# Heads of 8 in a gated four-layer block: weights times values on four column tiles, and a planner that knows VectorE's and POOL's shared port and the activation tables

## The chip, the cores and the metric

The kernel runs on one core of a Trainium2 chip. The metric is device time in microseconds (us) of that core; several runs are taken and their median is the kernel's time. Beside them one execution was recorded by the hardware profiler, and every duration of a single instruction comes from it.

## The reference

The input x is 16 batches of 128 tokens with 128 features; a context has 77 tokens with 96 features for each batch. Four layers follow one another, each a gated cross attention and a gated feed-forward part on the residual x:

- Layer 0: attention with 16 heads of 8 features, then a mixture of 8 experts of which each token takes 2 (gelu).
- Layer 1: attention with 16 heads of 64, then 8 linear experts weighted by a thresholded softmax.
- Layer 2: attention with one head of 128, then a mixture of 8 experts of which each token takes 1 (silu).
- Layer 3: attention with 16 heads of 8 again, then a feed-forward part with ternary weights, gelu and a layernorm.

The attention that the change touches (layers 0 and 3) is, for one batch:

```
q = (x @ wq + bq)  as 16 heads of 8        k, v = (y @ wk + bk), (y @ wv + bv)
attn = softmax(q k^T / sqrt(8), over the 77 context tokens)
out  = (attn v, heads side by side) @ wo + bo
```

The kernel works in float32 throughout.

## The kernel before, in words

**An order made by a planner.** The program is not emitted as it is written. Each call on an engine is recorded as an `Op` (`Program.record`, L200) with its inputs and outputs, an estimated duration (`_Engine.cost`, L457) and the engines that could run it; L441 is the one line through which nearly all of them are emitted, which is why the profile has nearly everything under L441 and why one goes by the names of tiles. `forward` (L251) then simulates the five engines: it repeatedly takes the ready operation with the smallest start time, plus a share of its duration for VectorE (`busy`), plus a small term for its place in the order (`bias`), if its tiles find free slots. `backward` (L351) turns the result round to get a new order, and `arrange` (L375) repeats both 8 times and keeps the shortest plan. The plan fixes engine, slot and order of every operation; the engines keep that order on the chip. Tiles of one tag share a fixed number of slots (L488), of which some are held back for older operations (`reserve`). The clock of TensorE is modelled (`_Clock`). The plan knows nothing of a port shared by VectorE and POOL, and nothing of ScalarE's loads of activation tables.

**Heads of 8** (`narrow_heads`, L741). Four groups of four batches. For a group: keys for all four batches in one product, spread by POOL into `kk`, in which each of the four heads of a 32-row band keeps its own 8 rows (a mask `hmask`); a layernorm of x (VectorE statistics, a power on POOL, `off_a` on VectorE, normalisation on VectorE or ScalarE), a transpose, the query product. For a batch, twice (halves `hf`, 8 heads each): two score products, one for each band of 32 rows (`sc`, 128 queries x 2 x 308 scores; 308 = 4 heads x 77); the maximum by head, the subtraction, and the exponential (`probabilities`, L668).

To multiply with the values, the weights have to be turned so that context tokens lie on partitions. 77 doesn't divide 128, so the subtraction writes its result split (`split`): first the tokens 0 to 63 of all 8 heads (512 columns), then the tokens 64 to 76 (104 columns), in two instructions. Four transposes of 128 columns give pairs of heads (`aT`), one of 104 the rest (`aTr`). The values lie in block matrices `vb` (`value_blocks`, L570, cleared once for each of the two layers by POOL; filled for each group by `narrow_values`, L714): a row for each token of a pair of heads, 9 columns for each head, the ninth being 1, so that the product gives the sum of the weights too. The product of weights and values (`av`, L795) has the turned weights as the stationary operand: 128 queries on partitions, five matmuls for each half, 10 for a batch. A reciprocal of 16 sums a row (`rs`) and one multiplication write `o`, four transposes a group turn it (`oT`), and the output product and a gated addition to x follow.

`narrow_values` loads the context in two arrangements (`ctxd`: tokens 0 to 63 twice; `ctxr`: tokens 64 to 76 eight times), one DMA of each for a group, in the queue of SyncE (SP), which also has the loads of the experts' columns and the stores of their results. For each batch two matmuls make the values, two copies put the first 64 tokens in place, one copy and a POOL multiplication with a mask (`rmask`) the rest.

Layer 0's groups are interleaved with its routing (L1503 to L1512); layer 3's with `ternary_ffn`, whose gelu needs another table than the exponential (L1539).

Of the kernel before, what the change touches and what calls it, by code (L numbers as in the profile page):

```python
# [11 lines left out]
F32 = mybir.dt.float32  # L12
# [15 lines left out]
KM = 64  # L28
KR = SK - KM
VW = 8 * 9  # L30
# [12 lines left out]
    ("cache", NE), ("hmask", 4), ("tri", NE * NE), ("rmask", 8),  # L43
# [102 lines left out]
class Op:  # L146
    def __init__(self, n, engines, us, after, order, size):
        self.n, self.engines, self.us, self.after, self.order = n, engines, us, after, order
        self.size, self.calls, self.deps, self.tiles = size, [], set(), []
        self.start = self.end = self.engine = None  # L150
        self.dense, self.streamed = 1.0, 0.0
# [26 lines left out]
class Program:  # L178
    LAG = {"tensor": 0.25, "vector": 0.08, "scalar": 0.08, "gpsimd": 0.1, "sync": 0.1}
    RATE = 290e3  # L180

# [18 lines left out]
    def record(self, engines, call, reads, writes, us, landing=0.0, group=None, size=0, streamed=0.0):  # L200
# [9 lines left out]
        op.streamed += streamed  # L210
        op.dense = min(1.0, op.streamed / max(op.us[0], 1e-3))
# [39 lines left out]
    def forward(self, order, ahead, bias, busy):  # L251
# [6 lines left out]
        holders = {tag: [None] * n for tag, n in self.slots.items()}  # L258
        held = {tag: [0.0] * n for tag, n in self.slots.items()}
        unplaced, out, wire, oldest = {}, [], 0.0, 0  # L260
        clock = _Clock()
# [28 lines left out]
        def place(op):  # L290

            at, got, taken = 0.0, [], {}
            for t in op.tiles:
                if t.slot >= 0:
                    continue
                frees = [
                    (held[t.tag][i], i) for i, h in enumerate(holders[t.tag])
                    if (h is None or h.left == 0) and i not in taken.get(t.tag, ())
                ]
                older = unplaced[t.tag][0] < t.nth  # L300
                if len(frees) <= (self.reserve.get(t.tag, 1) if older else 0):
                    return None
                when, i = min(frees)
                taken.setdefault(t.tag, set()).add(i)
# [4 lines left out]
        while len(out) < len(ops):  # L309
            best = None  # L310
            for n in ready:
                op = ops[n]
                got = place(op)
                if got is None:
                    continue
                if op.pos > oldest + ahead and got[1]:
                    if not any(t.left == 1 and t.slot >= 0 for t in op.tiles):
                        continue
                for e, when, us in zip(op.engines, op.when, op.us):
                    t = max(free[e], got[0], when)  # L320
                    key = (t + us * weigh[e] + bias * (op.pos - oldest), op.pos)
                    if best is None or key < best[0]:
                        best = (key, op, e, t, got[1], us)
# [5 lines left out]
            free[e] = op.end  # L329
            if op.after:  # L330
                wire = max(wire, op.end) + op.size / self.RATE
                op.end = wire + op.after
            for tl, i in got:
                tl.slot = i
                holders[tl.tag][i] = tl
# [7 lines left out]
            for tl in op.tiles:  # L343
                tl.left -= 1
                if not tl.left:
                    held[tl.tag][tl.slot] = max(u.end + self.LAG[u.engine] for u in tl.users)
# [28 lines left out]
    def arrange(self, rounds=8, ahead=300, bias=0.0008, busy=0.5):  # L375
# [23 lines left out]
    def emit(self, pools):  # L399
        order = self.arrange()  # L400
        with self.tc.manual_schedule():
            for op in order:
# [5 lines left out]
                for call in op.calls:  # L408
                    call(engine)

# [5 lines left out]
class _Engine:  # L416
# [5 lines left out]
    def __getattr__(self, what):  # L422
        def recorded(*args, group=None, covers=None, **kw):
# [24 lines left out]
            if self.names[0] == "tensor":  # L448
                moved, passes = (args[2], 1) if what == "transpose" else (kw["rhs"], 2)
                streamed = passes * n_of(moved) / 1200 * moved.shape[0] / 128  # L450
            return self.prog.record(
                self.names, call, reads, writes, us, costs[0][1], group, costs[0][2], streamed
# [4 lines left out]
    def cost(self, engine, what, args, kw, out):  # L457
        if "dma" in what:
            src = kw.get("in_", args[1] if len(args) > 1 else None)
            size = 4 * min(int(np.prod(v.shape)) for v in (out, src))  # L460
            if what == "indirect_dma_start":
                return 1.27, 2.2, 65536
# [6 lines left out]
        if engine == "gpsimd":  # L469
            if ALU.pow in args:  # L470
                return 0.8 + 0.06 * n, 0.0, 0
            return 0.12 + n / (1200 if what == "memset" else 440), 0.0, 0
# [4 lines left out]
        return 0.16 + n / 960 + (0.05 if what == "scalar_tensor_tensor" else 0.0), 0.0, 0  # L477
# [3 lines left out]
def tile_gated_blocks(  # L481
    ctx: ExitStack, tc: tile.TileContext, x, ctxa, ctxd, ctxr, cols, rows, b2s, emb, wqo0, wkv0, wx0,
# [6 lines left out]
        "sc": 2, "bank": 4, "large": 11, "middle": 18, "kk": 6, "at": 4, "aTr": 2, "other": 2, "mv": 3,  # L489
        "st": 4, "ve": 3, "rstd": 3, "mx": 4, "rs": 4, "rs1": 4, "rs2": 4, "junk": 2, "ys": 4,  # L490
        "back": 6, "wT": 1, "vr": 2, "off": 3,
    }
    reserve = {"sc": 1, "bank": 2, "large": 4, "middle": 6, "kk": 2, "at": 2}
# [62 lines left out]


    def pair_values(vb, par):

        flat = vb[KM * par : KM * (par + 1), 9 * par : 9 * par + 10 * VW]  # L560
        return flat.rearrange("p (c w) -> p c w", c=NH // 2)[:, :, :9]

    def rest_values(vb):

        flat = vb[: 8 * KR, : 10 * VW].rearrange("p (r w) -> p r w", r=2)[:, :, 4 * VW :]
        return flat.rearrange("p r (h d) -> p r h d", d=9)

    VB = 9 * VW + P

    def value_blocks(layer):  # L570
        whole = sb.tile([P, GB * VB], F32, tag="vb", name=f"vb_{layer}")
        nc.gpsimd.memset(whole, 0.0)
        got = []
        for i in range(GB):
            vb = whole[:, i * VB : (i + 1) * VB]
            for par in range(2):
                nc.gpsimd.memset(pair_values(vb, par)[:, :, 8:9], 1.0)
            nc.gpsimd.tensor_copy(
                rest_values(vb)[:, :, :, 8],
# [1068 lines left out]
```

## Time and profile before

| | us |
|---|---|
| three runs | 832.29, 835.16, 835.72; median 835.16 |
| profiled execution | 800.28 |
| its span, first to last instruction | 798.5 |
| granted TensorE clock | 0.944 of full speed |
| TensorE busy with matmuls | 701.5 |
| VectorE / ScalarE / POOL busy | 511.0 / 443.6 / 261.8 |
| ACT_TABLE_LOAD, 28 in all | 1.283 each |

The profiled execution took 34.9 us less than the median of the runs. A row of the profile's groups has the engine, the operation, the tile written and those read, the shape, the count, then the busy time in us and the mean of one in ns, then the idle time before it and what ended it. A matmul in float32 shows as two passes of TensorE (PE) with a weight load (PEld) each, a transpose as one. A row in order of time has the start, the duration and the number of instructions merged in it. By stages: layer 0's attention and routing lie at 0 to about 165 us, its experts to about 260, layers 1 and 2 to about 560, layer 2's experts to about 620, and layer 3 from there to the end.

### The profile page before, as it was taken

The page shows a single profiled execution, that of the slowest core. Times are in us where ns is not written, and L with a number is a line of the kernel's source. Part 1 is how long each engine was busy: PE and PEld are TensorE (multiplying, and loading weights), DVE is VectorE, ACT ScalarE, POOL GpSimd, SP SyncE. Part 2 cuts the span into 40 slices and gives each one's busy share as a digit, 9 for nine tenths or more (in the row PEclk, how much of TensorE's full clock was granted, in tenths as well). Part 3 has the DMA queues.
Part 4 walks back from the last instruction along what each step waited for, and adds up shares of the span by engine and source line. Part 5 has one row for each costly group of instructions (what it writes and reads, how often), then busy time and mean ns, then how long its engine had stood idle before and what let it go on. Part 6 is the DMA issues. An engine that isn't in the chain of part 4 may idle for free.

```text
span 798.5 us, 13848 instructions
## 1 busy us (share of the span) xinstructions
PE 701.5 (88%) x4848; PEld 555.7 (70%) x4848; DVE 511.0 (64%) x1462; ACT 443.6 (56%) x980; POOL 261.8 (33%) x327
## 2 busy tenths in 40 slices
PE   5699949999799998899899999878869977999886
PEld 3477837898687686568557767457859764867774
DVE  5868797482232664696769685675544796675864
ACT  3456525665456964565455555455636656556663
POOL 6511236107531222763322252461272260201010
PEclk9699969999999999999999999988989998979999
DMA  5005006387596100000000013500647100000000
GB/s 160 22 30 152 2 29 233 117 273 279 169 335 220 38 1 21 23 25 2 0 1 2 5 47 121 197 1 11 254 133 253 47 20 1 1 1 1 1 28 27
DMA packets 43541, 65.49 MB, mean 82 GB/s; under 512 B 4544, under 2 KB 32032, under 8 KB 43472
## 3 DMA queue, kind: packets, MB, share of 16 engines
q1 hardware_dynamic: 37520, 54.26, 20.6%
q0 software_dynamic: 3840, 9.31, 3.9%
q10 hardware_dynamic: 2112, 1.05, 0.5%
q8 instruction: 38, 0.62, 0.3%
q14 instruction: 31, 0.25, 0.1%
HBM read 52.41 MB, written 12.19 MB: 81 GB/s over the span
## 4 chain that ended last, share of the span: by engine, by line
PE 46%; DVE 10%; ACT 9%; issue 3%; POOL 2%; DMA 0%; POOLq 0%; ACTq 0%; DVEq 0%
PE sc_a L441 6%; PE aT_ps_a L441 6%; PE av_a L441 4%; PE oT_ps_a L441 4%; PE k_ps_a L441 4%; PE y_a L441 4%; PE y_ps L441 4%; PE y_f L441 3%; PE v_ps_a L441 3%; PE h_ps L441 3%; ACT L441 3%; DVE x L441 2%; POOL x L441 1%; ACT part_f L441 1%; PE h_ps_f L441 1%
## 5 line engine op out<-in xcount | busy, mean ns | idle before, releaser
L441 ACT ACTIVATE h<-h_ps,wx 128x128 f32<-128x128 f32 x304 | 86.4, 374 | 62.6 <-PE h_ps L441 52.6
L441 DVE TENSOR_REDUCE mx_a<-sc_a 128x8 f32<-128x616 f32 (+1 forms) x100 | 77.6, 776 | 28.6 <-PE sc_a L441 27.3
L441 ACT ACTIVATE at_a<-at_a 128x616 f32<-128x616 f32 (+1 forms) x100 | 70.4, 707 | 45.3 <-DVE at_a L441 42.9
L441 ACT COPY aT_a<-aT_ps_a 128x512 f32<-128x512 f32 (+1 forms) x124 | 70.1, 583 | 43.9 <-PE aT_ps_a L441 42.8
L441 DVE TENSOR_TENSOR at_a<-sc_a,mx_a 128x104 f32<-128x104 f32 (+3 forms) x164 | 83.9, 534 | 9.4 <-issue 4.0
L441 PE MATMUL h_ps<-rowsT,wx 128*128 128x128 f32 x608 | 83.9, 286 | 5.5 <-ACT h L441 3.4
L441 PE MATMUL aT_ps_a<-ident,at_a 128*77 128x128 f32 (+1 forms) x528 | 81.3, 288 | 6.3 <-ACT at_a L441 4.6
L441 PEld LDWEIGHTS h_ps<-rowsT,wx 128*128 128x128 f32 x608 | 77.0, 200 | 10.5 <-ACT h L441 4.8
L441 PE MATMUL y_ps<-wx,h 128*128 128x128 f32 x608 | 79.3, 278 | 3.7 <-DVE y L441 1.4
L441 PEld LDWEIGHTS aT_ps_a<-ident,at_a 128*77 128x77 f32 (+1 forms) x528 | 63.8, 150 | 24.6 <-ACT at_a L441 8.0
L441 PEld LDWEIGHTS y_ps<-wx,h 128*128 128x128 f32 x608 | 73.7, 194 | 7.0 <-DVE rowsT L441 1.6
L441 PE MATMUL av_a<-vb,aT_a 128*128 128x128 f32 x512 | 74.9, 293 | 2.3 <-ACT aTr_a L441 2.3
L441 PEld LDWEIGHTS av_a<-vb,aT_a 128*128 128x128 f32 x512 | 68.4, 207 | 8.3 <-ACT aTr_a L441 3.4
L441 PE MATMUL sc_a<-kk_a,q_a 32*128 32x308 f32 (+1 forms) x288 | 55.6, 492 | 16.8 <-DVE at_a L441 13.5
L441 POOL DMA_INDIRECT sorted_x<-xn_f,idx_f x48 | 46.7, 972 | 63.3 <-DVE r_both_f L441 29.8
L441 POOL TENSOR_TENSOR at_a<-at_a,rs_a 128x616 f32<-128x616 f32 x32 | 39.0, 1224 | 80.7 <-DVE rs_a L441 42.5
L441 POOL DMA_INDIRECT back_f<-sorted_y,idx_f x48 | 46.3, 965 | 57.3 <-DMA cf_a<-in_ctxd 26.1
L441 DVE TENSOR_TENSOR y<-y_ps,wx 128x128 f32<-128x128 f32 x76 | 21.5, 288 | 58.4 <-PE y_ps L441 27.9
L441 POOL TENSOR_TENSOR rstd_f<-ve_f,nhalf 128x4 f32<-128x4 f32 x16 | 16.3, 1019 | 112.2 <-DVE ve_f L441 104.1
L441 POOL TENSOR_TENSOR vb<-vr_a,cols_sb 104x128 f32<-104x128 f32 x32 | 14.0, 440 | 101.8 <-ACT vb L441 43.0
L441 PE MATMUL k_ps_a<-ctx_sb,wide_w 96*128 96x308 f32 x128 | 39.7, 446 | 5.8 <-ACT part_f L441 4.1
L441 PEld LDWEIGHTS sc_a<-kk_a,q_a 32*128 32x128 f32 (+1 forms) x288 | 23.6, 201 | 29.9 <-issue 10.4
(283 smaller groups left out, 1370.9 us busy)
## 6 DMA issues: line engine op xcount, KB each, us to landing
wx<-in_wx SPq DMA_DIRECT2D x60, 578.0 KB, 6.8
sorted_y<-y SPq DMA_DIRECT2D x76, 64.0 KB, 1.6
rows<-sorted_x SPq DMA_DIRECT2D x6, 512.0 KB, 3.9
sorted_x<-zero POOLq DMA_DIRECT2D x2, 1472.0 KB
cf_a<-in_ctxd SPq DMA_DIRECT2D x8, 224.0 KB
rows<-sorted_x SPq DMA_DIRECT2D x4, 448.0 KB
co_a<-in_ctxr SPq DMA_DIRECT2D x8, 182.0 KB, 3.6
x<-in_x ACTq DMA_DIRECT2D x4, 256.0 KB
```

What stands on the lines that cost most here:

```text
L441: getattr(engine, f)(*(_real(a) for a in args), **done)
```

## The change

In the attention with heads of 8:

- The 4 x 77 = 308 pairs of head and token of one 32-row band (four heads) stay in natural order: `probabilities` subtracts in one instruction again, and the 308 columns are turned in chunks of 128, 128 and 52 (`CHUNKS`). For a batch that makes 8 transposes of 128 columns as before and four of 52 instead of two of 104; the last four are evicted as one 52 x 512 copy.
- The values become the stationary operand, 32 columns wide (4 heads x 8 features), masked so that each row counts for its own head only; each band has one of four column tiles of TensorE, that is 32 partitions of the output. The sums of the weights come from a second product with the mask itself (`own`). For a batch: 2 x 3 chunks x 4 tiles = 24 matmuls. The output has features on partitions already, so `o` and its transposes are gone. The reciprocal now covers 128 elements a row, and the multiplication writes `oT`.
- `narrow_values` loads, for each batch, the context repeated over the 308 rows (`ctx4`, 112 x 384, one DMA a batch), makes the values with three matmuls, evicts them in one copy of 384 elements and masks them on POOL (384 elements). `value_blocks` is gone. Tag "v3" (9 slots) holds context, values and masked values.

In the planner: operations on POOL (other than DMA), and those of VectorE that read or write no PSUM and whose name begins with tensor or scalar (not tensor_reduce), can't overlap in the plan; an activation of another table than the last starts 1.28 us later; when nothing fits the reserves, the oldest operation may go without them. `rounds` 8 to 16, `bias` 0.0008 to 0.002, `busy` 0.5 to 0.3; some estimated durations; "middle" has 15 slots in place of 18.

```diff
-    def probabilities(scores, n, scale, name, split=None):
+    def probabilities(scores, n, scale, name):
...
+        nc.vector.tensor_tensor(at_v, scores, wide, ALU.subtract)
         nc.scalar.activation(at, at, AF.Exp, scale=scale)
...
+    def narrow_values(g, wv, n):
+        got = []
         for b in range(GB):
+            at = (g * GB + b) * PK
+            cx = sb.tile([KP, 3 * P], F32, tag="v3", name=f"cx_{n}_{b}")
+            nc.sync.dma_start(cx, ctx4[:, at : at + 3 * P])
+            vp = mm_tile(f"v_ps_{n}_{b}")[:, : 3 * D]
...
+            vr = sb.tile([P, 3, 4, 32], F32, tag="v3", name=f"vr_{n}_{b}")
+            evac(vr, vp.rearrange("p (c k d) -> p c k d", c=3, k=4))
+            vb = sb.tile([P, 3, 4, 32], F32, tag="v3", name=f"vb_{n}_{b}")
...
+            nc.gpsimd.tensor_tensor(vb, vr, mask, ALU.mult)
...
+                with nc.together(1.4):
+                    for sums in range(2):
+                        for c in range(3):
+                            for k in range(4):
+                                a = (chunks[k] + [aT[:, k, :]])[c]
+                                w = ones_of[:, c, :] if sums else vbs[b][:, c, k, :]
+                                nc.tensor.matmul(
+                                    av[32 * k : 32 * k + 32, sums * P : (sums + 1) * P],
+                                    lhsT=w[: a.shape[0]], rhs=a, start=(c == 0), stop=(c == 2),
+                                )
+                rs = sb.tile([P, S], F32, tag="rs", name=f"rs_{n}_{b}")
+                nc.vector.reciprocal(rs, av[:, P : 2 * P])
+                nc.vector.tensor_tensor(oT[:, b, :], av[:, :P], rs, ALU.mult)
...
+                        if e in op.port:
+                            t = max(t, port)
+                        if op.table not in (None, table):
+                            t += self.LOAD
...
-    def arrange(self, rounds=8, ahead=300, bias=0.0008, busy=0.5):
+    def arrange(self, rounds=16, ahead=300, bias=0.002, busy=0.3):
...
-        "sc": 2, "bank": 4, "large": 11, "middle": 18, "kk": 6, "at": 4, "aTr": 2, "other": 2, "mv": 3,
+        "sc": 2, "bank": 4, "large": 11, "middle": 15, "kk": 6, "at": 4, "v3": 9, "mv": 3,
```

## The prediction

> **What bounds the kernel now.** I read the engine shares first, then the chain of work that ended last, then the groups by shape, and last the order of time in two short stretches.
>
> ```profile
> PE 701.5 (88%) x4848; PEld 555.7 (70%) x4848; DVE 511.0 (64%) x1462; ACT 443.6 (56%) x980; POOL 261.8 (33%) x327
> ...
> PE 46%; DVE 10%; ACT 9%; issue 3%; POOL 2%; DMA 0%; POOLq 0%; ACTq 0%; DVEq 0%
> PE sc_a L441 6%; PE aT_ps_a L441 6%; PE av_a L441 4%; PE oT_ps_a L441 4%; PE k_ps_a L441 4%; PE y_a L441 4%; PE y_ps L441 4%; PE y_f L441 3%; PE v_ps_a L441 3%; PE h_ps L441 3%; ACT L441 3%; DVE x L441 2%; POOL x L441 1%; ACT part_f L441 1%; PE h_ps_f L441 1%
> ```
>
> TensorE is the bound, but not wall to wall: 88% counts overlapping passes. Summing, from the starts in the trace, what lies between one pass's streaming (0.85 ns a column) and the next start gives about 169 us in which no matmul streams; 19 of them lie before 40 us, 14 in the routing at 100 to 120, 15 at 640 to 680. So there are two kinds of time to win: TensorE's streaming in the attention with heads of 8, and gaps that the order leaves. The nameless ACT entry (3%; 2.7% in the chain's own answer, so 21.6 us) is table loads.
>
> An fp32 matmul shows as two passes. This is the product of values and weights of the kernel before, in order of time:
>
> ```profile
> 44.38 1.06 PE L441 MATMUL av_a<-vb,aT_a 128*128 128x128 f32 x8
> 45.27 0.39 PE L441 MATMUL av_a<-vb,aTr_a 104*128 104x128 f32 x2
> ```
>
> Eight passes start in 45.27-44.38 = 0.89 us, 0.111 each. A batch has 10 matmuls, 20 passes: 2.22 us, 71 us in 32 batches. The chain holds av_a for 4.4%, 35 us: half of it is on the path. The wide heads already put a product on two column tiles:
>
> ```profile
> 276.85 1.09 PE L441 MATMUL oT_ps_a<-aT_a,v_a 77*64 77x128 f32 x16
> 277.87 0.66 PE L441 MATMUL aT_ps_a<-ident,at_a 128*77 128x128 f32 x4
> ```
>
> Sixteen passes of the same 128 columns in 1.02 us: 0.064 each with entry and exit, so two tiles do run side by side. Inside the group the starts come in pairs, every 0.109 us.
>
> **VectorE's rows.**
>
> ```profile
> L441 DVE TENSOR_TENSOR at_a<-sc_a,mx_a 128x512 f32<-128x512 f32 x64 | 43.5, 680 | 0.1
> ...
> L441 DVE TENSOR_TENSOR at_a<-sc_a,mx_a 128x616 f32<-128x616 f32 x32 | 25.2, 788 | 1.2
> ...
> L441 DVE TENSOR_TENSOR at_a<-sc_a,mx_a 128x104 f32<-128x104 f32 x64 | 16.9, 265 | 8.0 <-issue 4.0
> ...
> L441 DVE RECIPROCAL rs_a<-av_a 128x16 f32<-128x16 f32 x32 | 8.1, 254 | 31.6 <-PE av_a L441 31.4
> ...
> L441 DVE RECIPROCAL rs_a<-rs_a 128x8 f32<-128x8 f32 x32 | 6.5, 203 | 1.1
> ```
>
> The reciprocal is the row to stare at: 203 ns for 8 elements a row, 254 for 16, 164 for 2: 6.4 ns for each further element, where the subtraction pays about 1.
>
> **VectorE against POOL, and table loads.**
>
> ```profile
> 25.04 5.21 DVE L441 SCALAR_TENSOR_TENSOR off_a<-mv_a,rstd_a 128x4 f32<-128x4 f32 x1
> 30.18 0.68 DVE L441 TENSOR_TENSOR at_a<-sc_a,mx_a 128x512 f32<-128x512 f32 x1
> ```
>
> ```profile
> 24.33 1.26 POOL L441 TENSOR_TENSOR x<-x,bos 128x512 f32<-128x512 f32 x1
> 25.55 2.24 POOL L441 TENSOR_TENSOR kk_a<-kr_a,cols_sb 128x1232 f32<-128x1232 f32 x1
> 27.76 2.47 POOL L441 TENSOR_TENSOR x<-x,bos 128x512 f32<-128x512 f32 x2
> ```
>
> ```profile
> L441 ACT ACT_TABLE_LOAD x27 | 34.6, 1283 | 1.3 <-PE h_ps L441 0.9
> ```
>
> A four-element operation (163 ns as a rule) lasts 5.21 us and ends when POOL's run ends at 30.23; behind it the next subtraction, and TensorE, stand (PE waits 5.8 us for at_a there). Over the run, VectorE's operations are 25 us longer than the usual time of their own shape in off_a (12.8), xn_a (5.6), x<-back (5.1) and ve_a (2.1).
>
> **What the skill says.** The Trainium skill, SBUF — State Buffer, "Who interferes with whom": a VectorE instruction with two SBUF inputs contends with a GpSimd one that reads SBUF, and the loser blocks fully; the 5.21 us agree. VectorE: DVE Perf Modes, "First, the fixed hardware budget": reciprocal is an iterative divide with a repeat count of 8; 6.4 ns an element agrees in kind. TensorE: Matmul & The Clock Gate, Part 3, "Measured speedup vs the span model": three column tiles of 32 gave 2.38 times; the trace shows two tiles only. ScalarE: Activation LUTs, "What ACT_TABLE_LOAD costs": 1283 ns and a drain of about as much; the row has the 1283, the drain no row shows.
>
> **The change part by part** (per batch, 32 batches; the sum is against the profiled 800.28 us, span 798.5).
>
> 1. *Product on four tiles.* 24 matmuls, 48 passes. If four run at once: 12 x 0.109 = 1.31 instead of 2.22: -0.91. Bounds: two at once 2.62, none 5.2. I take four: the two-tile group overlaps fully from its first pair. Transposes of the rest go from 2 to 4: +0.22; value projection from 4 passes to 6: +0.22; the transpose of o (4 a group) goes: -0.11; entering and leaving tile mode: after the tiled score group at 41.43 us the next weight load starts 0.09 us late and its pass takes 0.05 longer, and the load at entry has nothing to hide under: +0.2. Sum -0.38, 12 us in all; half on the path, like av_a now: **-6** (bounds +24 with pairs, worked out below, and -12).
> 2. *VectorE.* Two subtractions become one: 680+265-788 = 157 ns, twice: -0.31. The reciprocal goes from 16 to 128 elements: 254 + 112 x 6.4 = 0.97 us, +0.72. The product with it stays 290 ns. Net +0.40, 12.8 us. The planner prices the long reciprocal at 0.17+128/960 = 0.30, so each comes 0.67 late in a strict queue; behind it stand the next maxima and subtractions, and for those ScalarE's exponentials. VectorE has a third of slack in these stages (131 of 198 us busy after 600), so I put 0.4 on the path: **+5** (0 to +19).
> 3. *Evictions.* Values: 218+213+265 ns become one of 384 elements, about 480 between the 265 (128) and 583 (512) of ScalarE's rows: -0.22. The rest of the weights: 371 to 583: +0.21. oT: 583 a group: -0.15. **-1**; ScalarE and VectorE share it.
> 4. *POOL.* The masking goes from 128 elements (440 ns) to 384; 1232 take 2259, so 1.65 ns an element: 860 ns, +13.5 us. Gone are the clears of the value blocks (5.4+1.7+1.5 us), which ended at 5.6 us, before x arrives at 6.7: no gain there. POOL is 33% busy: **0**; uncovered, the first group pays 4 x 0.42.
> 5. *DMA.* 8 loads of 224 KB and 8 of 182 become 32 of 168: 2.1 MB more, 8 us of wire at the 279 GB/s of a full slice, and 16 more issues in SP's queue, each waiting for one of 9 slots; behind a waiting one stand expert columns and stores of y. Covered by loading ahead: **+1** (0 to +6).
> 6. *Planner, VectorE and POOL apart:* of the 25 us, 40% on the path (5.8 at 25 us and 3.6 at 650 are seen there): **-10** (0 to -25; it may also hold back work that never collided).
> 7. *Planner, table loads:* 28 now. One to start, gelu, exp, silu, exp, and two for each of four groups at the end make 13. I let 10 go, 12.8 us, 60% on the path (21.6 of 35.9): **-8** (0 to -15).
> 8. *Fewer buffers* ("middle" 18 to 15), other weights, more rounds: unknown, -10 to +10, taken as 0.
>
> Sum -6+5-1+0+1-10-8 = -19: 781 us profiled. The runs' median of 835.16 lies 34.9 above the profiled execution; I carry that over: **816 us**.
>
> **The rivals.**
> - *The tiles run only in pairs.* A matmul's two passes share a tile, so a queue that looks one instruction ahead finds only one neighbour. For: the trace shows no more than pairs. Against: with two tiles it couldn't show more. Then av costs 24 x 0.109 = 2.62, TensorE +0.93 a batch, 30 us, now as the bound 0.8 on the path: +24. With the other terms (-13): +11, **846**, slower. It decides from av = 2.22+0.67-0.53 = 2.36 us a batch (0.67 x 32 x 0.8 = 17 eats the 13 and the 0.5%).
> - *The reciprocal is on the path* whole: 23-4 = +19 instead of +5: **830**. For: each batch's tail runs through it, and the queue is strict. Against: VectorE's third of slack.
> - *The planner wins nothing*, its new estimates don't come true, and the smaller pools cost 10: -1+10: **844**.
> - *The planner wins all:* -25 and -15 instead of -10 and -8: **794**. For: 169 us of gaps.
>
> **The numbers.** Forecast 0.46 (own range 802 to 830), all won 0.19, reciprocal 0.15, pairs 0.11, planner nothing 0.09. A measurement here can tell about 0.5%, 4.2 us. Faster: 0.455+0.19+0.10 = 0.745, say 0.75. Same: 0.005+0.05+0.03 = 0.08. Slower: 0.10+0.07 = 0.17. The range 788 to 842 leaves out 0.07 below and 0.12 above.
>
> **What would show it.** av in order of time: 48 passes in about 1.5 us confirm step 1, 2.6 the pairs. RECIPROCAL rs_a 128x128 near 970 ns, and waits of mx_a or at_a behind it, step 2. off_a near 163 ns and no 5 us wait of PE, step 6. The count of table loads near 18, step 7. Gaps of TensorE before 40 us and at 640 to 680 still there would refute 6 and 7; SP waiting on v3 slots, step 5. The prediction is wrong if av is over 2.36 us, or if the new order opens gaps elsewhere.

## The result, and the profile after

The kernel after takes 831.04 us (median of 20 runs, 824.6 to 841.7), the kernel before 835.64 beside it (20 runs, 830.65 to 843.05): a ratio of 0.9938, 95% interval 0.9908 to 0.9967. The forecast was 816. The direction held; the size did not: a gain of 5 us where 19 were summed.

One thing has to be known of the numbers below. Chips differ: the kernel before takes 801 to 803 us on two of those used here and 835 on a third and in the runs shown. Its profiled execution (800.28) fits the faster kind alone, since none of its 20 executions beside the kernel after is under 830; the profile of after (826.01) is of the slower kind. The two pages can therefore not be subtracted from one another; ratios and profile pairs are taken within one kind of chip.

The page of after, its engine shares and its chain of what ended last:

```profile
PE 710.9 (86%) x5840; PEld 534.8 (65%) x5840; DVE 513.9 (62%) x1364; ACT 429.4 (52%) x932; POOL 272.3 (33%) x302
...
PE 68%; DVE 14%; DMA 5%; issue 4%; ACT 3%; another core or an unknown queue 3%; POOL 2%; DVEq 0%; POOLq 0%; SPq 0%; ACTq 0%
```

TensorE is still the longest, the nameless ACT entry (table loads) has left the chain, and 5% of DMA is new in it. The product of values and weights of one batch, in order of time (start, duration, matmul passes merged):

```profile
60.54 0.65 PE L462 MATMUL av_a<-aT_a,vb_a 128*32 128x128 f32 x16
61.12 0.42 PE L462 MATMUL av_a<-aTr_a,vb_a 52*32 52x128 f32 x8
61.47 0.64 PE L462 MATMUL av_a<-aT_a,own 128*32 128x128 f32 x16
62.04 0.42 PE L462 MATMUL av_a<-aTr_a,own 52*32 52x128 f32 x8
62.40 0.66 PE L462 MATMUL aT_ps_a<-ident,at_a 128*128 128x128 f32 x4
62.53 0.96 DVE L462 RECIPROCAL rs_a<-av_a 128x128 f32<-128x128 f32 x1 [0.66 <-PE av_a L462]
```

From the first of the 48 passes to the next other work are 1.86 us (60.54 to 62.40), where 20 passes took 2.22 and step 1 had 1.31 with 0.2 for entering and leaving. The groups that the prediction named (count, busy us, mean ns, idle before):

```profile
L462 DVE TENSOR_TENSOR at_a<-sc_a,mx_a 128x616 f32<-128x616 f32 x96 | 76.1, 794 | 5.8 <-PE aT_ps_a L462 1.1
...
L462 POOL TENSOR_TENSOR vb_a<-vr_a,own 128x384 f32<-128x384 f32 x32 | 32.8, 1033 | 51.9 <-ACT vr_a L462 33.9 <-DVE vr_a L462 15.4 <-PE v_ps_a L462 2.2
L462 DVE RECIPROCAL rs_a<-av_a 128x128 f32<-128x128 f32 x32 | 30.6, 956 | 26.7 <-PE av_a L462 26.6
...
L462 ACT ACT_TABLE_LOAD x17 | 21.8, 1283 | 4.4 <-PE h_ps L462 4.1
...
L462 DVE SCALAR_TENSOR_TENSOR off_a<-mv_a,rstd_a 128x4 f32<-128x4 f32 x16 | 2.6, 160 | 6.6 <-POOL rstd_a L462 6.6
```

Read one by one they say that the change does what it was said to do: one subtraction of 794 ns, a reciprocal of 956 (970 were estimated), 18 table loads (17 and one on another line) where there were 28, and off_a back at 160 ns with no 5 us stall in it. The prices on VectorE were about right; the product (1.86 us) and POOL's masking (1033 ns instead of 860) were priced too low. The larger question is what the operations are worth where they stand.

### The profile page after: what moved, and what is told of

It is laid out like the page before. It is cut to its first block, busy times and chain, and to the rows that moved or that the text cites. A ratio compares the mean times of both kernels' runs of the same rounds, so it can differ in the third digit from the quotient of the medians.

```text
span 824.0 us, 15717 instructions
## 1 busy us (share of the span) xinstructions
PE 710.9 (86%) x5840; PEld 534.8 (65%) x5840; DVE 513.9 (62%) x1364; ACT 429.4 (52%) x932; POOL 272.3 (33%) x302
## 4 chain that ended last, share of the span: by engine, by line
PE 68%; DVE 14%; DMA 5%; issue 4%; ACT 3%; another core or an unknown queue 3%; POOL 2%; DVEq 0%; POOLq 0%; SPq 0%; ACTq 0%
PE sc_a L462 8%; PE aT_ps_a L462 8%; PE av_a L462 8%; PE h_ps L462 7%; PE y_ps L462 6%; PE v_ps_a L462 6%; PE k_ps_a L462 5%; PE y_a L462 4%; PE oT_ps_a L462 4%; DMA wx<-in_wx 4%; PE y_f L462 3%; DVE x L462 2%; PE aTr_ps_a L462 2%; PE h_ps_f L462 2%
## 5 line engine op out<-in xcount | busy, mean ns | idle before, releaser
L462 PE MATMUL h_ps<-rowsT,wx 128*128 128x128 f32 x608 | 90.4, 302 | 29.6 <-DVE y L462 10.4
L462 PEld LDWEIGHTS h_ps<-rowsT,wx 128*128 128x128 f32 x608 | 83.1, 214 | 34.7 <-DVE y L462 11.9
L462 ACT COPY aT_a<-aT_ps_a 77x512 f32<-77x512 f32 (+1 forms) x118 | 66.7, 583 | 63.8 <-PE aT_ps_a L462 61.1
L462 DVE TENSOR_REDUCE mx_a<-sc_a 128x8 f32<-128x616 f32 (+1 forms) x100 | 77.6, 777 | 21.8 <-PE sc_a L462 21.4
L462 PE MATMUL y_ps<-wx,h 128*128 128x128 f32 x608 | 84.2, 291 | 5.8 <-DVE y L462 4.6
L462 PEld LDWEIGHTS y_ps<-wx,h 128*128 128x128 f32 x608 | 78.8, 205 | 8.8 <-issue 6.1
L462 DVE TENSOR_TENSOR at_a<-sc_a,mx_a 128x616 f32<-128x616 f32 (+1 forms) x100 | 78.0, 782 | 6.0 <-PE aT_ps_a L462 1.1
L462 PE MATMUL sc_a<-kk_a,q_a 32*128 32x308 f32 (+1 forms) x288 | 51.8, 468 | 16.3 <-DVE at_a L462 12.6
L462 POOL TENSOR_TENSOR vb_a<-vr_a,own 128x384 f32<-128x384 f32 x32 | 32.8, 1033 | 51.9 <-ACT vr_a L462 33.9
L462 DVE RECIPROCAL rs_a<-av_a 128x128 f32<-128x128 f32 (+1 forms) x40 | 31.8, 795 | 28.9 <-PE av_a L462 28.7
L462 PE MATMUL sc_a<-kk_a,xnT_a 128*128 128x308 f32 x128 | 38.5, 430 | 0.3 <-issue 0.2
```

The costliest lines, as they stand in the source:

```text
L462: getattr(engine, f)(*(_real(a) for a in args), **done)
```

## The experiments

The order on every engine is the planner's, and any edit that it can see (an operation, a price, a rule) makes it draw up a new one. All times are medians in us; the kernel before ran beside each.

| chip | before | kernel | us | ratio (95%) |
|---|---|---|---|---|
| one | 803.23 | b_again (before unchanged) | 802.09 | 0.9999 (0.9971 to 1.0027) |
| one | | planner_only | 763.77 | 0.9520 (0.9473 to 0.9566) |
| one | | heads_only | 812.62 | 1.0151 (1.0091 to 1.0212) |
| one | | recip_priced | 782.05 | 0.9763 (0.9710 to 0.9815) |
| two | 801.15 | planner_only_2 | 764.48 | 0.9548 (0.9511 to 0.9586) |
| two | | heads_only_2 | 811.76 | 1.0117 (1.0059 to 1.0174) |
| two | | after_3 (whole change) | 789.06 | 0.9874 (0.9833 to 0.9915) |
| two | | recip_priced_2 | 783.15 | 0.9790 (0.9747 to 0.9833) |
| two | 803.21 | planner_only_3 | 764.16 | 0.9508 (0.9459 to 0.9557) |
| two | | planner_long | 783.66 | 0.9761 (0.9714 to 0.9807) |
| two | | plan_no_port_2 | 795.67 | 0.9896 (0.9842 to 0.9949) |
| two | | plan_no_table_2 | 783.65 | 0.9740 (0.9701 to 0.9779) |
| one | 802.76 | planner_nudged | 780.29 | 0.9725 (0.9668 to 0.9782) |
| one | | after_nudged | 803.39 | 1.0029 (0.9999 to 1.0059) |
| three | 834.94 | after_again (whole change) | 828.52 | 0.9916 (0.9888 to 0.9944) |
| three | | recip_copy | 824.04 | 0.9880 (0.9827 to 0.9933) |
| three | | plan_no_port | 833.73 | 0.9985 (0.9958 to 1.0011) |
| three | | plan_no_table | 829.54 | 0.9933 (0.9914 to 0.9953) |

### The two parts apart

*b_again* is the kernel before, *planner_only* has the change's planner, estimates and weights with the attention and the buffers of before, *heads_only* the reverse:

```diff
 # planner_only                        # heads_only
-    def forward(...)   # of before    -    narrow_heads, narrow_values, probabilities   # of before
+    def forward(...)   # of after     +    narrow_heads, narrow_values, probabilities   # of after
```

> The kernel before, unchanged, for a second profile of it. Theory 1 (the profiled 800 us was a rare, lucky execution, in which the experts' columns came in time): its usual profile spans about 833 us, and the 33 us stand in the two expert stages as waits of TensorE for loads, so that the stage from the first gelu to the wide heads lasts some 125 to 140 us instead of 113. Theory 2 (the gap is the clock or something outside the program): the span is about 833 us with every stage longer by the same 4%.

> Only the planner's part of the change (shared port, tables, new weights, rounds and estimates), with the attention of before. Theory A (my sum: planner -18 us, attention -1): 0.975 to 0.985 of before. Theory B (the new orders give back in the expert stages what the attention wins): 1.00 to 1.02, with the table loads down to about 18 and the long off_a gone all the same.

> Only the attention's part (four column tiles, one subtraction, long reciprocal, 32 loads of context), planned by the planner of before. Theory A: 0.995 to 1.005, TensorE's gain and the reciprocal cancelling. Theory B: 0.97 to 0.985, the attention being the gain and the new planner the loss. Theory C (the reciprocal, priced by the planner at a third of its time, is the loss): 1.00 to 1.02.

The first says what one profile of the kernel before is worth: 802.09 us beside 803.23, with a profiled span of 806.3, so neither of its theories held, and the 34.9 us between profile and runs that I carried over were a difference between chips. The other two split the result: the planner alone wins 39.5 us (0.952, outside both of its theories), over twice the 18 that steps 6 to 8 gave it, and the attention part costs 9.4 (in Theory C's range) where steps 1 to 5 gave it a gain of 1.

That had to be repeated with the whole change on the same chip: *after_again*, meant for chip one, fell on chip three, and so the whole change had run only where the kernel before takes 835 us:

> The planner's part of the change with the attention of the kernel before, once more, on the same chip as the whole change and the attention part alone. On a chip where the kernel before took 803 us it stood at a ratio of 0.952. Theory A (the two parts get in each other's way: the attention part costs about 1.5%, and it spoils the plan as well): the ratio is 0.95 to 0.96 on this chip too, and the whole change stands 3% or more above it. Theory B (the gain of the planner's part depends on the chip, because the chips differ in what the stages of the experts take): on a chip where the kernel before takes about 835 us the ratio is 0.97 to 0.99, and the whole change stands at most 1.5% above it. Rival: the plan of this kernel is lucky on that one chip, and the ratio is here within 0.5% of 1.

> The attention part of the change with the planner of the kernel before, on the same chip as the whole change. It stood at a ratio of 1.015 where the kernel before took 803 us. Theory A (its cost comes from the order that it brings, not from the chip): 1.01 to 1.02 here too. Theory B (chip decides): within 0.5% of 1, or under it. If the parts add, the whole change is the product of this ratio and that of the planner's part alone; if they spoil one another the whole change is over 1% above that product.

> The whole change, unchanged, on the same chip as its two parts. If the parts add, its ratio is the product of theirs: with those of the earlier chip 0.952 x 1.015 = 0.966. It stood at 0.994 and at 0.992 where the kernel before took 835 us. Theory A (the parts spoil one another): 0.985 or more, and over 1% above the product of the two parts measured here. Theory B (chip decides): within 1% of the product of the two parts measured here, whatever that is.

> The changed kernel, unchanged, on the chip of these experiments, where the kernel before takes 803 us instead of 836. If the planner's part and the attention's part only added up (0.952 and 1.015), it is at 0.967. If the attention's long reciprocal upsets the new plan in particular, it stays near the 0.994 of the result. If the result's chip is what held it back (slower loads of expert columns), it falls between 0.965 and 0.98 and TensorE's gaps at 140 to 200 us shrink from 45 us in four slices of 20 to some 15.

The planner's part: 36.7 us won; the attention part alone: 10.6 lost; both: 12.1 won. The ratios of the parts multiply to 0.966, the whole stands at 0.987. So on top of the new planner the attention part costs 24.6 us (3.2%), not 10.6: in these orders the parts do not add. The chip is not the explanation, as all three were measured on chip two. Whether the parts get in each other's way, or three orders merely fell differently, this comparison can't tell; the section on the draw comes back to it.

Where the time is lost shows in the trace when the span is cut in three: to the first expert product of layer 0 (attention with heads of 8, and routing), from there to the last expert product of layer 2, and the rest (layer 3, heads of 8 again). Busy time of each engine by stretch (start and end, length, then busy us and instructions of TensorE, its weight loads, VectorE, ScalarE and POOL, then the granted clock of TensorE, the DMAs' share and GB/s), first planner_only_2:

```profile
0.00:131.20 131.20, 117.76 (x804) 92.26 (x805) 99.67 (x298) 70.39 (x154) 53.99 (x76) 0.95 0.33 108
131.20:616.20 485.00, 438.93 (x3091) 351.53 (x3089) 286.73 (x860) 260.33 (x634) 174.04 (x216) 0.95 0.31 101
616.20:766.90 150.70, 138.96 (x957) 107.90 (x956) 110.91 (x304) 94.57 (x181) 31.99 (x35) 0.94 0.05 15
```

and after_3, the whole change on the same chip:

```profile
0.00:137.60 137.60, 117.23 (x1307) 76.61 (x1307) 109.59 (x260) 69.62 (x132) 61.74 (x66) 0.94 0.36 111
137.60:623.10 485.50, 435.67 (x3054) 348.73 (x3055) 281.00 (x840) 257.15 (x625) 167.51 (x198) 0.94 0.31 101
623.10:786.40 163.30, 145.22 (x1482) 98.51 (x1480) 124.46 (x267) 102.31 (x176) 43.03 (x39) 0.93 0.08 22
```

The profiled spans differ by 19.5 us: 6.4 in the first stretch, 12.6 in the last, 0.5 between. Two profiles of one kernel scatter too: planner_only_3, the same kernel on the same chip as planner_only_2, has 134.5, 481.2 and 150.0, so only the last stretch stands clear. VectorE has 9.9 and 13.6 us more to do at the two ends and 5.7 less in the middle.

TensorE's side has to be counted from the starts. At 0.85 ns a column, as in the prediction, its passes stream 588.8 us in planner_only_2 and 576.5 in after_3, 12.3 less. But the time between the first pass and the last in which none streams grows from 163.3 us to 195.5, and it has two parts. Gaps under 150 ns, mostly the passes' own, grow from 71.5 to 84.2, by 12.7; the longer ones from 91.7 to 111.3, by 19.6. So the streaming that the four tiles saved was taken back by short gaps, and TensorE needs as much as before (660.3 and 660.7 us; 659.9 and 660.1 in the two kernels of the section on the draw). Where these gaps lie shows in one batch: the tiled product's first pass starts 0.20 us after the pass before it instead of 0.11 (medians), and it then takes 1.85 us against 2.23, which leaves 0.28 of the 0.71 us that were forecast. The attention's other passes (two transposes and two value passes more, one transpose less) take about as much, 0.33 us by the prediction's own prices.

The long gaps are as large as the loss in time, and some of them are slow passes: the granted clock is recorded at full speed or at half, and at half passes of 128 columns start 213 ns apart instead of 112 (medians of passes in a row in after_3). planner_only_2 spends 76.7 us at half, after_3 96.7; what they stream there would take 32.2 and 40.5 us at full, so some 8 us more are lost that way (an estimate from these figures; 6 against planner_only_3). Whether the clock falls because TensorE waits, or for another reason, no run separates. One place of the waits is visible in the score products, which wait for VectorE to give their PSUM buffer back. In planner_only_3:

```profile
L463 PE MATMUL sc_a<-kk_a,q_a 32*128 32x308 f32 (+1 forms) x288 | 55.6, 485 | 7.5 <-DVE at_a L463 7.5
```

and in after_3:

```profile
L462 PE MATMUL sc_a<-kk_a,q_a 32*128 32x308 f32 (+1 forms) x288 | 52.9, 476 | 16.9 <-DVE at_a L462 13.5 <-ACT q_a L462 3.4
```

This wait belongs to the order: the kernel before has 13.5 us of it as well, and recip_priced_2, with the same long reciprocal, 3.4.

heads_only differs in place: its 807.5 us of span are 142.1, 496.5 and 168.9, beside 148.9, 479.4 and 170.2 in the page of before and 149.3, 487.9 and 169.1 for b_again. Under the old planner the new attention is 7 us *faster* in its first stage, about even in its second, and 9 to 17 us slower between them, where only a few of its operations (layer 3's first keys, values and scores) run. That was the first sign that an order drawn anew has a price of its own.

### The reciprocal

*recip_priced* tells the planner what the reciprocal takes; *recip_copy* replaces it by a copy, so that the output is multiplied by the sums and not divided by them, with the plan of the whole change left exactly as it is:

```diff
 # recip_priced, in _Engine.cost
+        if what == "reciprocal":
+            return 0.15 + 0.0064 * n, 0.0, 0
 # recip_copy
-                nc.vector.reciprocal(rs, av[:, P : 2 * P])
+                nc.vector.tensor_copy(rs, av[:, P : 2 * P])
```

> The changed kernel with the reciprocal priced in the plan as measured (0.15 us and 6.4 ns an element, so 0.97 us for 128) instead of 0.30. Theory C (late reciprocals upset the plan): 0.975 to 0.985 of before. Theories A and B: what the changed kernel has, 0.99 to 1.00, give or take the 1% that another order brings.

> The whole change with one number of the plan altered, the reciprocal's cost at 0.15 us and 6.4 ns an element in place of 0.30 us, on the same chip as the whole change. It stood at 0.976 where the kernel before took 803 us. If the wrong price is what spoils the plan, this stands 1.5 to 3% under the whole change, near the product of the two parts. If a price merely draws another order by lot, it stands within 1% of the whole change, on either side.

> The changed kernel with a copy of the sums in place of their reciprocal, so the result of the attention is multiplied by the sums instead of divided: the plan is the same to the last operation, but the step takes about the 0.29 us that the plan gives it, not 0.96. It takes 21 us of VectorE away. Theory C (the unplanned reciprocal is on the path and upsets the order): 15 to 25 us less than the changed kernel. Theory A (0.4 of it is on the path): 8 us less. If VectorE had slack throughout: under 4 us less.

With the true price the whole change comes to 783.15 instead of 789.06 us on the same chip (782.05 on chip one), 5.9 us or 0.7% better, with intervals that touch at 0.9833. That is within the 1% that was foretold for a mere new order, so the wrong price is not shown to cost anything. Its last stretch, 148.9 us, is as short as planner_only_2's with the long reciprocal in it; its middle, 493.7, is 8.2 longer than after_3's. The copy lasts 291 ns instead of 956, 21.3 us less of VectorE in 32 batches, and the time falls by 4.5 (828.52 to 824.04, intervals overlapping): in an order that stays as it is, on chip three, about four fifths of the reciprocal lie in slack. That is what step 2 had claimed. *planner_long* adds the long reciprocal, and nothing else of the attention part, to the best kernel; seven of its eight results are not used:

```diff
-                rs = sb.tile([P, 2, 8], F32, tag="rs", name=f"rs_{n}_{b}")
-                nc.vector.reciprocal(rs, av[:, :, :, 8])
+                rs = sb.tile([P, 2, 8, 8], F32, tag="rs", name=f"rs_{n}_{b}")
+                nc.vector.reciprocal(rs, av[:, :, :, 1:9])
...
-                    rs[:, :, :, None].to_broadcast([P, 2, 8, 8]), ALU.mult,
+                    rs[:, :, :, 7:8].to_broadcast([P, 2, 8, 8]), ALU.mult,
```

> The planner's part with the attention of the kernel before, in which the reciprocal takes in 128 elements a row in place of 16 (seven of eight are not used): 0.70 us more on VectorE for each of 32 batches, 22.5 in all, and nothing else of the attention part. VectorE is 85% busy in the two stages with heads of 8 (112 of 131 us, 124 of 151). Theory V (VectorE is the bound there, and the step of the prediction that put the reciprocal at 0.4 us a batch from its slack is the one that failed): 12 to 20 us over the whole planner's part, ratio 0.97 to 0.98, and the stages to the first expert product and from the last one 6 to 10 us longer each. Theory W (the long reciprocal lies in slack, and the attention part loses by something else: the later first product, table loads of its plan, the order): under 6 us over it, ratio under 0.963.

The added operation in planner_long, and its three stretches:

```profile
L463 DVE RECIPROCAL rs_a<-av_a 128x128 f32<-128x128 f32 x32 | 30.5, 953 | 14.2 <-PE av_a L463 14.1
```

```profile
0.00:138.70 138.70, 118.79 (x811) 91.34 (x812) 112.29 (x288) 71.67 (x161) 54.09 (x76) 0.95 0.33 102
138.70:624.00 485.30, 430.96 (x3100) 345.71 (x3099) 290.19 (x867) 264.65 (x639) 177.30 (x217) 0.96 0.31 101
624.00:776.90 152.90, 138.06 (x942) 107.99 (x940) 115.67 (x293) 95.86 (x185) 29.72 (x34) 0.95 0.05 15
```

783.66 beside 764.16: 19.5 us slower for 22.3 more of VectorE (953 less 255 ns, 32 times). By time that is Theory V. By place it is not: the profiled execution, 11.3 us over planner_only_3's, has 4.2 of them in the first stretch, 4.1 between and 3.0 in the last, and against planner_only_2 7.5, 0.3 and 2.2, where 6 to 10 were expected at either end. The expectation's "85% busy" was too high as well: the stretches of planner_only_2 give 99.67 of 131.20 (76%) and 110.91 of 150.70 (74%). So the long reciprocal was worth 4.5 us where the order was kept and 19.5 where the order was drawn anew around it, and the second figure includes whatever the new order is worth by itself.

### The planner's rules

planner_only without the shared port, and without the table loads:

```diff
 # plan_no_port                                # plan_no_table
-                        if e in op.port:      -                        if op.table not in (None, table):
-                            t = max(t, port)  -                            t += self.LOAD
```

> The attention of before with the new planner, but VectorE and POOL may overlap in the plan. My step 6 (the port's 25 us, 40% of it on the path): 10 us more than planner_only, 0.964 of before, and off_a of several us is back. If the port is nearly all of the planner's 39 us: 0.99. If it is none: 0.952.

> The attention of before with the new planner, but table loads cost nothing in the plan. My step 7: 8 us more than planner_only, 0.962 of before, and about 28 table loads instead of 16. If the tables are nearly all of the gain: 0.99. If none: 0.952. What neither this nor plan_no_port loses belongs to the other weights, rounds and estimates.

> The planner's part without the rule that keeps VectorE and POOL apart, beside the whole planner's part. Step 6 of the prediction put the rule at 10 us, so 1.2% over the whole planner's part; on another chip it stood at 0.9985. Theory A (the rule carries most of the gain): 2.5% or more over the whole planner's part, most of it before the first expert product and in the four-element off_a. Theory B (any change of the plan throws the middle stages about by 10 us or more): over 2.5%, but with the attention stages of 8 heads within 3 us and the difference in stages that have none of the collisions.

> The planner's part without the rule that counts table loads: 34 loads in place of 16, 18 x 1.28 = 23 us of ScalarE. Step 7 of the prediction put 10 loads at 8 us, so 14 us for 18 (1.7%) over the whole planner's part. Theory A (the loads are mostly on the path): 2 to 4% over it. Theory B (they lie in ScalarE's slack): under 1%.

On chip two, beside planner_only_3, the kernel without the port rule takes 31.5 us more and the one without the table rule 19.5; on chip three both stood close to the kernel before (0.9985, 0.9933), but the full planner's part did not run there, so no price follows from those two. Between the two chips the ratio of each rises by 1 to 2%, with intervals apart, so a ratio is not free of the chip either. The table rule's reading is straightforward. ScalarE's loads without it:

```profile
L461 ACT ACT_TABLE_LOAD x33 | 42.3, 1283 | 1.4 <-DVE at_a L461 0.5 <-issue 0.3
```

34 loads (33 and one elsewhere) against 16, 23.1 us of ScalarE more and 19.5 on the clock, and TensorE's waits that ScalarE ends grow from 23.0 us to 40.0 (waits over 150 ns). The port rule's reading is not. Summing what each VectorE operation takes over the median of its own shape gives 17.4 us with the rule and 24.1 without: 6.7 us of collisions do not make 31.5. off_a, which was to be several us long again, lasts 171 ns without the rule. And the loss lies in the middle stretch, 513.3 us instead of 481.2, while the first is 4.0 longer and the last 2.2 shorter. Part of the middle is layer 3's attention, begun earlier in this order (TensorE streams 9.6 us more in the middle and 9.8 less in the last stretch); that it started earlier made the last stretch hardly shorter. The clock is at half for 88.7 us of that middle instead of 37.5. That is about what Theory B of that run foretold: a different order.

### How much is the draw

Last, the planner's weight for a place in the order was altered by a twentieth in both kernels; rules, prices, buffers and operations stay:

```diff
-    def arrange(self, rounds=16, ahead=300, bias=0.002, busy=0.3):
+    def arrange(self, rounds=16, ahead=300, bias=0.0021, busy=0.3):
```

> The planner's part with the attention of the kernel before, with the weight bias at 0.0021 in place of 0.002: the same rules, prices, buffers and operations, and another order on every engine. The unnudged plan stood at 0.951, 0.952 and 0.955. Theory R (the rules carry the gain): 0.945 to 0.962. Theory L (the order is a draw, and that plan was a lucky one): 0.965 or more, with most of the difference in the stages between the first and the last expert product, which hold none of the changed attention.

> The whole change with the weight bias at 0.0021 in place of 0.002, and nothing else. The unnudged whole change stood at 0.987 beside the two parts, and with another price for the reciprocal at 0.976 and 0.979. Theory R (the attention part costs 3% under the new planner): 0.980 to 0.995, and 2.5% or more over the nudged planner's part. Theory L (draws): anywhere from 0.96 to 1.00, and the two nudged kernels under 2% or over 4.5% apart.

The planner's part goes from 764 to 780.29 us, the whole change from 789.06 (chip two) to 803.39 (chip one), which is no gain any more over the kernel before. So two orders of one kernel lie 14 to 16 us apart, about 2%, and planner_only's was the better of its two; how wide the whole spread is, two orders don't tell. The nudged planner's part has 20 table loads instead of 16, and off_a is back at 455 ns on average, with both rules in the plan. Theory L had the range of the planner's part right, and neither theory that of the whole change: 1.0029, 3% above the nudged planner's part. Where Theory L put the difference is not to be read from stretches that scatter by 3 to 8 us between profiles of one kernel; for the whole change most of it is in the middle (12.9 longer).

The distance between the two kernels is 23.1 us nudged, 24.6 unnudged, and 18.7 with the reciprocal priced (783.15 less 764.48). But nothing ties the order of one kernel to that of the other. Taken crosswise, two orders of the planner's part against three of the whole change (one with the reciprocal priced), the distance is anything from 2 to 39 us, some 20 on average. All six have the same sign: the attention part costs time under the new planner, and how much is known no better than that.

What it waits for is clearer. These are TensorE's waits of over 150 ns in us, by the engine that ended them:

| kernel | VectorE | ScalarE | POOL |
|---|---|---|---|
| planner_only_3 | 27.8 | 23.0 | 1.3 |
| planner_nudged | 37.9 | 26.0 | 1.2 |
| after_3 | 41.5 | 21.4 | 0.7 |
| recip_priced_2 | 50.9 | 21.5 | 1.2 |
| after_nudged | 52.3 | 19.2 | 1.2 |
| planner_long | 51.7 | 24.5 | 0.0 |

Every order with the long reciprocal waits more for VectorE than either order without it, and none waits more for POOL or, but for planner_long against planner_only_3, for ScalarE. Three profiles of planner_only's order lie between 27.2 and 28.0. That points at VectorE, to which the attention part adds work. It is no proof that the reciprocal is the cause: two orders without it, the kernel before (42.9) and plan_no_port_2 (45.5), wait as long for VectorE.

## Why the prediction was wrong, step by step

On the chips where the kernel before takes 801 to 803 us, as its profile did, the sum of -19 compares with a measured -12; on those of the runs shown with -5.

1. *Product on four tiles: right that four run at once, wrong in what TensorE saves.* The passes of four tiles start 7 ns apart, and fours follow one another every 0.109 us, so the rival of pairs is out. Entering and leaving cost the 0.2 us that were allowed. But the term left out 0.11 us more at each of three changes of row count, and 0.02 us more behind the first four of each of four blocks: the product takes 1.95 us with its entry, not 1.51. With these 0.44 us a batch, -0.38 becomes +0.06, and the step is worth nothing instead of -6.
2. *VectorE: the step that failed.* The prices were right (956 ns for 970), the share on the path was not. I took +5 out of bounds of 0 to +19, from "VectorE has a third of slack in these stages". Slack as an average says nothing of whether a long operation finds it in a strict queue: added by itself, in a new order, the reciprocal came with 19.5 us, taken out of a fixed order with 4.5, and under the new planner's rules TensorE waits longer for VectorE in every order that has it (41 to 52 us against 28 and 38). The upper bound that the prediction worked out for the rival of the reciprocal (+19) is close to what planner_long measured. VectorE also got more than the 0.40 us a batch: 17.7 us over the whole span where 12.8 were summed.
3. *Evictions:* 475 ns for 384 elements (480 estimated) and 579 for 52 x 512 (583). Right.
4. *POOL:* 1033 ns instead of 860. TensorE hardly waits for POOL itself (table above). The first product of weights and values in layer 0 starts at 26.6 us instead of 23.9 in the pair on chip two, of the order of the uncovered 4 x 0.42; but after_nudged starts at 22.0, so it is the order's as much as POOL's.
5. *DMA:* the context is covered, as assumed: TensorE waits for cx_a 1.7 us in all at most (after_nudged). Behind it the expert columns come late in one order: 11.1 us of waits for wx in after_3, against 3.2 in planner_only_3, 2.7 in after_nudged and none in recip_priced_2.
6. *VectorE and POOL apart: the 10 us not separable.* The sign that was named came true, TensorE's gaps before 40 us fall from 20.6 us to 9.9 in planner_only_2. VectorE's excess over the median of each shape falls from 29 us in the kernel before to 17 in planner_only_3, 12 and not 25. off_a is cured, but not by this rule alone: it is short without it (171 ns) and long again with it in planner_nudged (455 ns). Most of the rule's 31.5 us is not collisions.
7. *Table loads:* 18 predicted, 18 counted; 16 without the attention part. 60% was put on the path, and 19.5 us for 23.1 us of loads were measured, with a draw's uncertainty of the same size.
8. *Other weights and buffers: "-10 to +10, taken as 0" was too narrow.* A twentieth of one weight moves 16 us. What the smaller pools alone cost was not measured.

The prediction's 169 us in which no matmul streams comes to 195 when it is counted again from the same starts; no term of its sum rests on it.

So two errors of opposite sign made the forecast look closer than its parts: the planner won 37 to 39 in its better order (about 22 in the other) instead of 18, and the attention part lost about 20 on top of it instead of winning 1. The third error is the base: the 34.9 us added at the end were chip against chip. That hid that the runs shown came from a chip on which the change is worth less.

Three things stay open. How the attention part's loss divides between the long reciprocal, POOL's mask, the smaller pools ("middle" 15 slots for 18, "rs" 2 for 4) and the order is not settled: planner_long's 19.5 could be the reciprocal alone, but a draw is worth nearly as much. Whether the four tiles would pay with fewer changes of row count and a relieved VectorE was not tried. And the cause of the chips' difference is unknown: the same plan takes 137.6, 485.5 and 163.3 us in its stretches on chip two and 146.5, 515.4 and 163.1 on chip three, so all of it lies before the last expert product.

The best version seen is the change's planner with the attention of before: 764 us, 0.951 to 0.955 of the kernel before in three measurements, 0.9725 after the nudge. In its better order it beats every order of the whole change; nudged (780.29) it is level with the whole change with the reciprocal priced (782.05 on the same chip).

## What to carry to other kernels

Where an order is made by a planner, alter a weight by a twentieth and measure how far the time moves before reading anything into an edit: here it was 2%, more than the change itself gained. Price a tiled product with its entry, its exit and its changes of row count; here they took back all that the tiles saved in streaming. Price what an edit adds to an engine that feeds the busiest one as if it were on the path, and test it by adding that operation alone, in more than one order; an average of slack gave 5 us where the one order tried took 19.5. Compare a profile with runs only where the kernel before has the same time in both.

## What the runs showed of the hardware

- Column tiles with fp32 passes: within one row count of the stationary operand, four tiles start 7 ns apart and the next four 0.109 us later (0.133 for the first pair of fours). At each change between 128 and 52 rows the next four start 0.22 us later instead, three times a batch (60.89 to 61.12 us in the batch shown). Sorting the chunks by row count would leave one change of the three; that was not tried.
- A reciprocal of 128 elements a row takes 949 to 956 ns wherever it stands, a copy of the same PSUM tile 291.
- A table load takes 1283 ns in every row, and where nothing else holds ScalarE its next operation starts 11 or 12 ns later (in 25 of the 28 loads of the kernel before).
- The granted clock of TensorE is recorded at full speed or at half. At half, passes of 128 columns in a row start 213 ns apart (after_3, median), at full 112.
- The same kernel, in the same order, takes 5% longer on one chip than on another (after_3 789.06, after_again 828.52), with granted clocks of 0.940 and 0.925 in their profiled executions; the kernel before 4% (803.21 and 834.94).
